# A two-layer graph network: one more graph's queries in seven products, and the row of sums kept in its accumulator

## The chip, the cores and the metric

The kernel runs on one core of one Trainium2 chip, as a single launch. The metric is the device time in microseconds (us). The kernel before takes 2637.73 us, the median of 3 runs (2637.07 to 2638.66). All data are 32-bit floats.

## The reference, cut to what matters

There are B = 16 graphs of N = 1024 nodes with C = 256 features, 4 heads of 64, and one adjacency matrix for all.

```
# layer 0, per graph, on h = max(layernorm(x), 0)
c    = mean over the features of h                        # one number per node
A    = abs(abs(sigmoid(c_m - c_n) - 0.5) - 0.5) * 2       # 1024 x 1024
Wg   = adj * A                                            # weighted graph
g    = relu((h^T @ Wg) * para)                            # queries, 256 x 1024
k, v = split(h @ kv_w)
x    = x + softmax(q k^T * scale) v                       # 4 heads
# layer 1, on h = max(layernorm(x), 0)
A_hat = (adj + I) scaled by rsqrt of the degrees on both sides
out  = batchnorm(relu(batchnorm(A_hat h W1^T + b1)) W2^T + b2)
x    = x + out
```

The batch normalisations take their statistics over all graphs, so the last product waits until all graphs are through.

## The kernel before, in words

**Order.** The program is written out by hand, in one order, and each engine takes its instructions in that order. `attention()` (L969) walks through the graphs. A graph has 16 *steps*: two halves of the features (k), two halves of the nodes (f), and four groups of two tiles each. A k and f together are a *unit* of four steps. In a step `scores()` (L863) makes two pairs of score products, and ScalarE takes their exponentials into p (L879); `Unit.add` (L892) sums p into `acc` on VectorE; `Unit.values` (L903) multiplies the p of the step before with the values. Behind the last group of a unit comes `Unit.sums` (L923): TensorE sums `acc` over the partitions by a product with ones (L929), ScalarE copies the result to an SBUF tile `row` (L931), GpSimd's queue sends two rows of it to DRAM (L932) and loads them back with the nodes on the partitions (L937, two loads). `finish` (L941) and `add_output` (L952) turn the unit's output, take the reciprocal of those sums (L955), multiply and add to x. They come two steps after the sums, three in graph 0.

**Background.** Beside the attention of graph b runs `background(b)` (L775), a generator of *pieces*. A piece of four products costs 1.71 by the planner's count. After each step the planner takes pieces until their cost has reached a due value, which grows by the total divided by 16 in each step (in graph 0, 50.0 in all, 3.125 per step). `weave(main, *sides)` (L137) runs one slot of each side generator behind each piece of the main one, from a given piece on; sides left over when the main one ends run at once. `double` (L147) runs two slots at a time. `soon` puts an action off by one piece.

**What background(0) does.** It transposes h of graph 1 (`transposed`, L374), makes keys and values (`keys_values`, L602, four pieces for k and four for v), and the weighted graph by `weigh(1)` (L408): eight tiles w, each two Abs (L439) and one Tanh (L447) on ScalarE and one multiplication with adj on VectorE (L426). A tile's slots come in pairs. Then the queries of graph 1: `plain_queries` (L568) multiplies all of h with all of w, 32 products of 128 x 128 x 512 in 16 pieces, and VectorE multiplies by para (L593). For the graphs from 2 on `queries` (L467) does it with seven half-size products, Strassen's scheme in Winograd's form, in 14 pieces: VectorE combines parts of h (`combine`, L459), subtracts tiles of w from each other in place (`take`, L501) between the products, and combines the results. Its temporary s1 sits in a tag "s1" with one buffer, which `degrees` uses for its diagonal tiles db too (L222).

**Beside the queries of graph 1** run two sides. `degrees` (L213) loads eight row tiles of adj_t, takes row sums on ScalarE (L221) and diagonals on VectorE (L223, L224), and ends with a power on GpSimd. `graph` (L232) prepares the seven pieces of adj + I for layer 1, wholly on GpSimd: for each of eight units two loads on GpSimd's queue (L247), four subtractions (L266 to L271), three DMAs to DRAM (L273 to L275). It takes two tiles of the tag "y" per unit; that tag has four buffers, and `row` (L930) is of the same tag.

**After it** come `differences(2)`, the rest of `keys_values(1)` and `prepare(2)`. In the later graphs the background also has layer 1's `aggregate` and `hidden`. TensorE's bank tag "mm" has two buffers, "sc" two, "acc" two, "p" four, "adj" three.

Of the kernel before, what the change touches and what calls it, by code (L numbers as in the profile page):

```python
# [17 lines left out]
P = 128  # L18
# [5 lines left out]
def gnn_two_layers_kernel(  # L24
# [61 lines left out]
    def layers(shifted):  # L86
# [126 lines left out]
        def degrees():  # L213

            nc.vector.tensor_reduce(row, rows.rearrange("p q t -> p t q"), AX.X, ALU.add)
            ahead = [load_adj_t(t, "at") for t in range(2)]
            yield 0.0
            for t in range(NT):
                a = ahead[t]
                blk = a[:, t * P : (t + 1) * P]  # L220
                nc.scalar.activation(a, a, AF.Copy, accum_out=col[:, t : t + 1])  # L221
                db = p1.tile([P, P], F32, tag="s1", name=f"db_{t}")  # L222
                nc.vector.tensor_mul(db, blk, ident)  # L223
                nc.vector.tensor_reduce(diag[:, t : t + 1], db, AX.X, ALU.add)  # L224
                if t + 2 < NT:
                    ahead.append(load_adj_t(t + 2, "at"))
                yield 0.0
            nc.vector.tensor_add(deg, col, row)
            nc.vector.tensor_sub(deg, deg, diag)
            rsqrt(dinv, deg, 1.0, tmp_deg)  # L230
# [159 lines left out]
        def differences(b):  # L390


            cbc = p1.tile([P, N], F32, tag="cbc", name=f"cbc_{b}")
            cbcs[b] = (
                cbc.rearrange("p (t q) -> p t q", t=NT)
                if b == 0
                else cbc.rearrange("p (q t) -> p t q", t=NT)
            )
            weighers[b] = weigh(b)
            if b == 0:  # L400
                broadcast_row(cbc, columns_of(csums[b], f"c{b}"), f"c{b}")
                return
            nc.sync.dma_start(out=csum_d[b].rearrange("(p t) -> p t", p=P), in_=csums[b])
            nc.sync.dma_start(
                out=cbc, in_=csum_d[b].rearrange("(o n) -> o n", o=1).to_broadcast([P, N])
            )
# [161 lines left out]
        def plain_queries(b):  # L568

            h = hs["a", b]  # L570
            qs[b] = [p4.tile([P, N], F32, tag="q", name=f"q_{b}_{k}") for k in range(CC)]
            for q in range(NH):
                cols = slice(q * FB, (q + 1) * FB)
                pgs = [bank(f"pg_{b}_{q}_{k}") for k in range(CC)]
                paras = []
                for k in range(CC):
                    paras.append(p2.tile([P, FB], F32, tag="para", name=f"para_{b}_{q}_{k}"))
                    nc.sync.dma_start(out=paras[k], in_=para[k * P : (k + 1) * P, cols])
                for th in range(NP):
                    i = q * NP + th  # L580
                    for k in range(CC):
                        for j in range(TH):
                            t = th * TH + j
                            product(
                                pgs[k],
                                h[:, t, k * P : (k + 1) * P],
                                weighted[b][i][:, j, :],
                                t == 0,
                                t == NT - 1,
                            )  # L590
                        if th == NP - 1:
                            dst = qs[b][k][:, cols]
                            nc.vector.tensor_mul(dst, pgs[k], paras[k])  # L593

                            soon(
                                lambda dst=dst: nc.scalar.activation(
                                    dst, dst, AF.Relu, scale=SCALE
                                )
                            )
                        yield 1.71  # L600

        def keys_values(b):  # L602
            ht = hts[b]
            ks[b] = [p4.tile([P, N], F32, tag="k", name=f"k_{b}_{k}") for k in range(CC)]
            for g in range(NH):
                for j in range(CC):
                    cols = slice(g * FB, (g + 1) * FB)
                    pk = bank(f"pk_{b}_{j}_{g}")
                    for k in range(CC):
                        product(  # L610
                            pk, kvw[:, k, j * P : (j + 1) * P], ht[k][:, cols], k == 0, k == CC - 1
                        )
                    nc.scalar.copy(ks[b][j][:, cols], pk)  # L613
                    yield 1.71

            vs[b] = [p4.tile([P, NT, P], F32, tag="v", name=f"v_{b}_{k}") for k in range(CC)]
            for g in range(NT // 2):
                pv = bank(f"pv_{b}_{g}").rearrange("p (j c) -> p j c", j=2)
                for j in range(2):
                    t = 2 * g + j  # L620
                    for k in range(CC):
                        product(
                            pv[:, j, :],
                            ht[k][:, t * P : (t + 1) * P],
                            kvw[:, k, C : 2 * C],
                            k == 0,
                            k == CC - 1,
                        )
                for k in range(CC):
                    nc.vector.tensor_copy(  # L630
                        vs[b][k][:, 2 * g : 2 * g + 2, :], pv[:, :, k * P : (k + 1) * P]
                    )
                yield 1.71
# [141 lines left out]
        def background(b):  # L775

            if b == 0:
                differences(1)
                for k in range(CC):
                    yield TOP  # L780
                    transposed(1, k)
                    yield 1.0
                w, products, norm = weighers[1], keys_values(1), Norm(2, True).all()
                yield from weave(
                    islice(products, 4), (0, double(islice(w, 8))), (0, islice(norm, 4))
                )
                yield from weave(
                    plain_queries(1), (0, norm), (0, w), (5, graph()), (7, degrees())
                )
                differences(2)  # L790
                yield from islice(products, 2)
                yield from prepare(2, products)
                return
            before = hidden(b - 1)
            gather = aggregate(b - 1)
            if b + 1 < B:
                w, products, norm = weighers[b + 1], keys_values(b + 1), normed(b - 1)
                yield from weave(islice(products, 4), (0, islice(w, 4)))
                if b == 1:
                    load_later()  # L800
                yield from weave(queries(b + 1), (0, double(w)), (9, islice(norm, 5)))
                yield next(gather)
                yield from weave(products, (0, norm))
            else:
                yield from weave(endings.pop(), (2, normed(b - 1)))
                yield next(gather)
            if b + 2 < B:
                yield from weave(gather, (3, summed(b + 2)))
                yield from prepare(b + 2, before)
            elif b + 2 == B:  # L810

                yield from gather
                endings.append(before)
            else:
                yield from gather
                yield from weave(before, (0, normed_last()))
# [66 lines left out]
        class Unit:  # L883
# [39 lines left out]
            def sums(self):  # L923

                u = self.index
                pt = ps_t.tile([P, FB], F32, tag="t", name=f"sums_{self.name}")
                for e in range(2):
                    r = slice(e * HD, (e + 1) * HD)
                    nc.tensor.matmul(pt[r, :], ones, self.acc[:, e, :], start=True, stop=True)  # L929
                row = py.tile([P, FB], F32, tag="y", name=f"row_{self.name}")  # L930
                nc.scalar.copy(row, pt)  # L931
                nc.gpsimd.dma_start(  # L932
                    out=sums_d[u], in_=row.rearrange("(e r) c -> e r c", r=HD)[:, 0, :]
                )
                self.inv = p2.tile([P, FB // P, 2], F32, tag="inv", name=f"inv_{self.name}")
                for e in range(2):
                    nc.gpsimd.dma_start(  # L937
                        out=self.inv[:, :, e], in_=sums_d[u][e].rearrange("(j q) -> q j", q=P)
                    )
# [459 lines left out]
```

## Time and profile before

| | |
|---|---|
| median of 3 runs | 2637.73 us |
| profiled execution | 2634.44 us |
| its span | 2632.6 us |
| granted TensorE clock, mean | 0.99 |
| GpSimd's DMA issue L932, each | 0.59 us, x64 |
| GpSimd's DMA issue L937, each | 0.77 us, x128 |
| VectorE's subtraction of w tiles, L501 | 1.22 us, x112 (14 graphs of 8) |
| VectorE's product with para in plain queries, L593 | 0.68 us, x8 (2 graphs of 4) |
| attention of graph 0 on TensorE | 61.5 to 197 us |

The profile is one execution. In a group's line stand the source line, the engine, the operation, the tiles it writes and reads, its shapes and count, then the busy time in us, the mean in ns of one, and the idle time of the engine just before it with what ended most of it. A line of a timeline gives the start, the length (of several merged, from the first's start to the last's end), the instruction, and in brackets the idle time before it. A product in 32-bit floats shows as two matmul records for each half of the columns, so a piece of the queries is eight records. PE is TensorE, DVE VectorE, ACT ScalarE, POOL GpSimd, SP SyncE.

### The profile page before, as it was taken

The page shows a single profiled execution, that of the slowest core. Times are in us where ns is not written, and L with a number is a line of the kernel's source. Part 1 is how long each engine was busy: PE and PEld are TensorE (multiplying, and loading weights), DVE is VectorE, ACT ScalarE, POOL GpSimd, SP SyncE. Part 2 cuts the span into 40 slices and gives each one's busy share as a digit, 9 for nine tenths or more (in the row PEclk, how much of TensorE's full clock was granted, in tenths as well). Part 3 has the DMA queues.
Part 4 walks back from the last instruction along what each step waited for, and adds up shares of the span by engine and source line. Part 5 has one row for each costly group of instructions (what it writes and reads, how often), then busy time and mean ns, then how long its engine had stood idle before and what let it go on. Part 6 is the DMA issues. An engine that isn't in the chain of part 4 may idle for free. (4 is left out here: it accounts for less than half of the span.)

```text
span 2632.6 us, 31894 instructions
## 1 busy us (share of the span) xinstructions
PE 2555.9 (97%) x11754; PEld 937.9 (36%) x11754; DVE 1725.3 (66%) x2736; ACT 1440.5 (55%) x1905; POOL 547.9 (21%) x648
## 2 busy tenths in 40 slices
PE   8979999999999999999999999999999999999995
PEld 3333333333333333333333333333333333334443
DVE  5647575766757675757667575757576675557675
ACT  5756464737364564647374645556464744335544
POOL 1361111011111111110111111111111112036653
PEclk9999999999999999999999999999999999999997
DMA  4463415252433324152524343342425233455559
GB/s 162 136 214 104 153 61 181 84 179 82 152 101 141 104 97 148 59 186 77 180 81 152 101 150 102 109 135 66 176 73 180 81 137 97 132 196 207 193 182 378
DMA packets 137188, 364.02 MB, mean 138 GB/s; under 512 B 21440, under 2 KB 38336, under 8 KB 130880
## 3 DMA queue, kind: packets, MB, share of 16 engines
q1 hardware_dynamic: 110272, 282.70, 31.5%
q0 software_dynamic: 26752, 79.20, 8.7%
q8 instruction: 95, 1.56, 0.3%
q14 instruction: 69, 0.57, 0.1%
HBM read 287.06 MB, written 74.78 MB: 137 GB/s over the span
## 5 line engine op out<-in xcount | busy, mean ns | idle before, releaser
L879 ACT ACTIVATE p<-sc 128x1024 f32<-128x1024 f32 x512 | 495.0, 1020 | 470.3 <-PE sc L871 464.1
L901 DVE TENSOR_TENSOR acc<-acc,p 128x1024 f32<-128x1024 f32 x384 | 470.8, 1226 | 222.4 <-ACT p L879 202.1
L871 PE MATMUL sc<-q,k 64*128 64x512 f32 x2048 | 511.4, 618 | 14.3 <-ACT p L879 14.3
L912 PE MATMUL o<-p,v 128*64 128x512 f32 x2048 | 497.0, 606 | 0.0
L160 PE MATMUL pg<-w,h_a 128*64 128x512 f32 x1600 | 358.1, 592 | 3.6 <-ACT k L613 1.9
L160 PE MATMUL pa<-aht,h_b 128*64 128x512 f32 x1536 | 343.5, 592 | 0.0
L871 PEld LDWEIGHTS sc<-q,k 64*128 64x128 f32 x2048 | 176.2, 186 | 336.8 <-issue 278.7
L439 ACT ACTIVATE w<-cbc,csum 128x512 f32<-128x512 f32 x256 | 293.5, 1198 | 0.0
L932 POOL DMA_DIRECT2D sums_d<-row x64 | 37.6, 587 | 1199.8 <-ACT row L931 1199.8
L160 PE MATMUL py<-at,w 128*64 128x512 f32 x1024 | 230.4, 592 | 0.0
L912 PEld LDWEIGHTS o<-p,v 128*64 128x64 f32 x2048 | 124.6, 136 | 294.6 <-issue 293.9
L426 DVE SCALAR_TENSOR_TENSOR w<-w,adj 128x1024 f32<-128x1024 f32 x128 | 157.9, 1234 | 89.2 <-ACT w L447 85.2
L160 PEld LDWEIGHTS pg<-w,h_a 128*64 128x64 f32 x1600 | 115.6, 137 | 231.7 <-issue 216.9
L160 PEld LDWEIGHTS pa<-aht,h_b 128*64 128x64 f32 x1536 | 110.4, 137 | 213.3 <-issue 201.0
L726 ACT ACTIVATE y<-py,vec 128x512 f32<-128x512 f32 x128 | 87.7, 685 | 149.0 <-PE py L160 125.1
L730 DVE BATCH_NORM_STATS2 stats<-y 128x6 f32<-128x512 f32 x128 | 85.5, 687 | 86.2 <-ACT y L726 86.2
L898 DVE TENSOR_TENSOR acc<-p,p 128x1024 f32<-128x1024 f32 x64 | 78.9, 1232 | 92.3 <-ACT p L879 92.3
L447 ACT ACTIVATE w<-w 128x1024 f32<-128x1024 f32 x128 | 135.2, 1056 | 1.8
L501 DVE TENSOR_TENSOR w<-w,w 128x1024 f32<-128x1024 f32 x112 | 132.9, 1218 | 1.5
L727 POOL DMA_DIRECT2D y_d<-y x128 | 70.2, 549 | 303.3 <-ACT y L726 302.1
L937 POOL DMA_DIRECT2D inv<-sums_d x128 | 98.4, 772 | 147.0 <-issue 63.3
L160 PEld LDWEIGHTS py<-at,w 128*64 128x64 f32 x1024 | 74.2, 137 | 145.2 <-issue 139.5
(151 smaller groups left out, 2822.0 us busy)
## 6 DMA issues: line engine op xcount, KB each, us to landing
aht<-aht_d SPq DMA_DIRECT2D x224, 512.0 KB, 6.3
adj<-in_adj_dram SPq DMA_DIRECT2D x128, 512.0 KB, 4.2
y_d<-y POOLq DMA_DIRECT2D x128, 256.0 KB, 2.6
yin_f<-y_d SPq DMA_DIRECT2D x32, 1024.0 KB, 6.3
x<-in_x_dram SPq DMA_DIRECT2D x32, 512.0 KB, 5.0
para<-in_para_dram SPq DMA_DIRECT2D x64, 256.0 KB, 3.9
x_d<-x POOLq DMA_DIRECT2D x16, 1024.0 KB, 10.4
xo_f<-x_d SPq DMA_DIRECT2D x32, 512.0 KB, 8.6
```

What stands on the lines that cost most here:

```text
L160: nc.tensor.matmul(dst[r], left[:, r], right, start=start, stop=stop)
L426: nc.vector.scalar_tensor_tensor(w, w, 1.0, a, op0=ALU.add, op1=ALU.mult)
L439: nc.scalar.activation(w[:, t, :].rearrange("p (t q) -> p t q", q=P), cbc[:, q * NT // NH : (q + 1) * NT // NH], AF.Abs, bias=csum[:, th * ...
L447: nc.scalar.activation(made[i], made[i], AF.Tanh, scale=-0.5 / C)
L501: nc.vector.tensor_sub(block(i)[part], block(x)[part], block(y)[part])
L726: nc.scalar.activation(y, made, AF.Identity, bias=b1[:, j : j + 1])
L730: nc.vector.bn_stats(stats1[:, j, i, :], y)
L871: nc.tensor.matmul(sc[:, e, :], ks[b][k][r, m * P : (m + 1) * P], qs[b][k][r, f * FB : (f + 1) * FB], start=True, stop=True,)
L879: nc.scalar.activation(pr, sc, AF.Exp)
L901: nc.vector.tensor_add(self.acc, self.acc, pr)
L912: nc.tensor.matmul(self.o[r, :], vs[b][k][:, m, r], pr[:, e, :], start=(m == 0), stop=(m == NT - 1),)
L937: nc.gpsimd.dma_start(out=self.inv[:, :, e], in_=sums_d[u][e].rearrange("(j q) -> q j", q=P))
```

## The change

Three things change, in two places.

1. In `background(0)` the queries of graph 1 are made by `queries(1)` in place of `plain_queries(1)`: seven half-size products in 14 pieces, with their combinations on VectorE and two copies on ScalarE.
2. The weighted graph of graph 1 runs further ahead: its generator gets two slots behind each of the two transposes, then eight beside the four k pieces as before, and two (not one) per piece of the queries. `degrees` starts beside the fourth piece (3), not the eighth (7), `graph` beside the fifth (4), not the sixth (5). The slot order among the sides changes: w now comes ahead of the norm.
3. In `Unit.sums`, for all 64 units, the copy of the sums goes to the first half of `acc`, which has just been summed, and no "y" tile is taken. The DMA reads it there.

```diff
             if b == 0:
                 differences(1)
+                w, products, norm = weighers[1], keys_values(1), Norm(2, True).all()
                 for k in range(CC):
                     yield TOP
                     transposed(1, k)
                     yield 1.0
-                w, products, norm = weighers[1], keys_values(1), Norm(2, True).all()
+                    yield from islice(w, 2)
                 yield from weave(
                     islice(products, 4), (0, double(islice(w, 8))), (0, islice(norm, 4))
                 )
                 yield from weave(
-                    plain_queries(1), (0, norm), (0, w), (5, graph()), (7, degrees())
+                    queries(1), (0, double(w)), (0, norm), (3, degrees()), (4, graph())
                 )
...
                     nc.tensor.matmul(pt[r, :], ones, self.acc[:, e, :], start=True, stop=True)
-                row = py.tile([P, FB], F32, tag="y", name=f"row_{self.name}")
+                row = self.acc[:, 0, :]
                 nc.scalar.copy(row, pt)
```

## The prediction

> **What bounds the kernel now.** I first read the page's busy times and slices. TensorE is the bound over the whole span, but one slice among the early ones shows 7.
>
> ```profile
> PE 2555.9 (97%) x11754; PEld 937.9 (36%) x11754; DVE 1725.3 (66%) x2736; ACT 1440.5 (55%) x1905; POOL 547.9 (21%) x648
> ...
> PE   8979999999999999999999999999999999999995
> ...
> POOL 1361111011111111110111111111111112036653
> ```
>
> The slice with 7 (132 to 197 us) is the one in which POOL shows 6: graph 0's attention, beside which the second graph's queries, the degrees and `graph()` run. That is where both edits act. Next I cut it into windows of 8 us (columns: window, then length, busy PE, PEld, DVE, ACT and POOL, granted clock, DMA share, GB/s).
>
> ```profile
> 132.00:140.00 8.00, 8.00 (x38) 2.61 (x36) 0.00 (x0) 1.10 (x2) 6.65 (x11) 1.00 0.80 309
> ...
> 172.00:180.00 8.00, 0.84 (x8) 0.29 (x4) 0.00 (x0) 0.50 (x2) 7.44 (x12) 0.69 0.56 198
> 180.00:188.00 8.00, 6.93 (x24) 2.78 (x24) 5.54 (x7) 7.97 (x9) 6.49 (x9) 0.67 0.35 120
> ```
>
> From 172 to 180 everything stands but POOL. The timelines of ACT, PE, DVE and POOL say why (start, length, instruction, in brackets the idle time before it and what ended it):
>
> ```profile
> 138.90 0.59 ACT L931 COPY row<-sums 128x512 f32<-128x512 f32 x1 [8.93 <-DMA aht_d<-two]
> ...
> 179.50 0.59 ACT L931 COPY row<-sums 128x512 f32<-128x512 f32 x1 [13.40 <-POOL two L266]
> ```
> ```profile
> 162.68 1.08 PE L929 MATMUL sums<-acc,ones 128*64 128x512 f32 x4 [2.46 <-DVE acc L901]
> ...
> 181.06 3.79 PE L871 MATMUL sc<-q,k 64*128 64x512 f32 x8 [8.22 <-ACT p L879]
> ```
> ```profile
> 158.15 0.20 DVE L955 RECIPROCAL inv<-inv 128x8 f32<-128x8 f32 x1 [6.00 <-DMA inv<-sums_d]
> ```
> ```profile
> 143.46 0.58 POOL L932 DMA_DIRECT2D sums_d<-row  x1
> 151.38 1.56 POOL L937 DMA_DIRECT2D inv<-sums_d  x2 [7.34 <-DMA sums_d<-row]
> ...
> 185.44 0.64 POOL L932 DMA_DIRECT2D sums_d<-row  x1
> 187.43 1.54 POOL L937 DMA_DIRECT2D inv<-sums_d  x2 [1.35 <-DMA sums_d<-row]
> ```
>
> There are two chains. One: the copy of a unit's sums to `row` waits for a "y" buffer that `graph()` holds; the exponentials queue behind it on ACT, the scores behind those. Two: the sums' DMAs and the inverses' loads are queued on POOL behind `graph()`; DVE's reciprocal waits for them, the sums of p behind it, TensorE behind those. TensorE's idle gaps from 140 to 196 us are 1.69+0.33+2.46+8.22+0.48+0.76 = 13.9 us, and the lower clock makes the scores at 181 us 1.8 us longer than the usual 1.99 and the transposes behind them 0.3. From 196 us on it is full: windows of 160 us hold 159.6 to 159.8 busy until the attention's end.
>
> **What the Trainium skill says.** "TensorE: Matmul & The Clock Gate", Specifications: ScalarE, VectorE and GpSimdE are strict FIFO; the waits above agree. Same page, "What's actually happening": an idle window halves the clock; here it falls to 0.69 and 0.67 after the 8.22 us. "SBUF — State Buffer", "Who interferes with whom": a DVE instruction with two SBUF inputs and a GpSimd one that reads SBUF share a port pair, and the second to issue blocks fully. It agrees: beside L901 a L267 took 1.59 us instead of 0.73. "DMA: Bandwidth & Descriptors", "Anatomy of one DMA — SWDGE (gpsimd) path": some 2 us fixed, mostly the write receipt. Here `sums_d` lands in 1.7 us where it is quiet, in 7.6 behind `graph()`'s writes.
>
> **The change, part by part.** I number graph 0's attention in steps (one pair of score groups, then the values of the step before) and the unit sums by unit: sums 0 come in step 4, sums 1 in 8, sums 2 in 12, sums 3 in step 16. Three steps after its sums a unit needs its inverses. The planner's due is 3.125 per step.
>
> *Two pieces fewer.* Queries take 14 pieces in place of 16; two pieces are 3.60 us in PE's timeline (pg x16). So graph 0's pieces end about one step sooner.
>
> *DVE and ACT beside it.* Added: 8 subtractions of w by 1.22 (L501), 2 combinations by 0.69, 11 sums and differences by 0.69, 4 L487 by 0.68; removed: 4 L593 by 0.68. Net 9.8+1.4+7.6 = 18.7 us of DVE, and two copies (0.48 each in sequence) on ACT. From 76 to 140 us DVE is busy 32 of 64, and the later graphs carry the same work without a gap on PE, so this I cost at nothing on DVE. If the cover fails, DVE's lag lands on the wait for the inverses.
>
> *The weighted graph earlier.* Two pairs of slots move to steps 1 and 2, all the rest to Q0, Q1 and Q2. A pair is 3.35 us of ACT (2.39+0.96). ACT up to the exponentials of step 4: from 67.05 (end of step 1's) come 8 pairs 26.8, exponentials of steps 2 and 3 3.7, four k copies 1.9, three pairs of relu 3.5, two new copies 0.95: 103.9 against 101.46 now. So sums 0's copy comes 2.45 us later. TensorE's waits in steps 2 to 5 become 1.0+2.0+3.4+1.5 against 1.06+1.87+2.33; it runs about 2 us late by step 6. The moved loads of adj sit on SP, before para and `at`; cbc landed by 63.5 us, in time. The next graph's cbc and adj loads come to stand on SP two pieces earlier, near 146 to 158 us, beside `sums_d` 1: its landing stays as slow as now. `degrees()` and `graph()` start at pieces 3 and 4, not 7 and 5; at step 5 POOL still has the loads of inverses 0 ahead of them, so `graph()` starts at 108.23+2.45 = 110.7.
>
> *The copy into acc.* ACT no longer waits (8.93 and 13.40 us gone), nor do the exponentials. The copy itself costs the same. It holds an acc buffer until the DMA has read it, where it was free after TensorE's sums; the next user is the unit after next, four steps later, and for unit 1 that first sum (step 12) stands on DVE behind the inverses of unit 1 anyway, which land after `sums_d` 1. So nothing; if that cover were gone, the wait would be `sums_d`'s landing. Nothing else in the kernel waits for "row" (L931 elsewhere waits for its sums, at most 0.3 us).
>
> *What is late next.* POOL. Its chain is not shortened by the copy. Sums 1 (step 8) now come with `graph()`'s unit 5, not 4, behind them in POOL's queue: five units ahead in place of four. In this order:
> - units 0 to 3: 111.3 to 143.46 now, so +2.45 and half a collision: 146.4
> - unit 4: 6.4 now, 7.1 with a collision: 153.5
> - `sums_d` 1: landing 3 to 7.6 us after issue, I take 5.5: 159.0; loads of the inverses 1.56: 160.6; the second lands 5 after its start: 165 (161 to 167)
>
> TensorE has reached sums 2 at about 159.7 (its solid run to 142.6, K5 to 148.2, two steps). DVE stands from step 11 with everything behind the reciprocal: add_output 1.85, two sums 2.5; sums 2 start at 169 to 170. So TensorE waits about 10 us here in place of 2.46. On POOL goes on:
> - unit 5 8.3 (10.2 now with two collisions), unit 6 7.1, unit 7 5.7, the degrees' power 2.3, one collision 1: 185.0
> - `sums_d` 2, its landing, both loads: second load starts at 187.8, lands 3.1 later: 190.9
> - add_output 1.85, two sums 2.5: **sums 3 at 195.2**, now 198.35
>
> TensorE and ACT alone would be there at 192.5: from 170 come sums and K8 (4.5 at the low clock), the three slots and exponentials on ACT to 179, 183.4 and 187.4, then scores, transposes and values. The later of the two counts: 198.35-195.2 = 3.1 us gained. After sums 3 both kernels have the same work, all of it on a full TensorE, so the 3 us stay.
>
> **Sum.** The profiled execution took 2634.44 (span 2632.6 and 1.8 around it); 2631.4 after. The median of the runs is 3.3 us above that execution, so 2637.7-3.1 = 2634.6. About 0.2% (5.3 us) is what a measurement of this kernel tells from no change.
>
> **Rivals.** *Full credit*: the gaps vanish and nothing takes their place: 13.9+2.1 idle and slow clock, 3.6 of pieces, less 2.5 of new ACT waits: 17.1 us, 2620.6. For it: ACT's waits are the larger ones named. Against it: POOL is busy from 108 to 185 us almost without a gap, and DVE waits for what hangs on it. A weaker form (POOL's landings short) stops at the TensorE path, 2632.
>
> *POOL longer* (slower): 18.7 us more of two-input DVE work runs while POOL subtracts. Each collision costs POOL about 0.95. Now 5.6 us of its chain are collisions. With every second of its 32 subtractions hit it is 15.2, 9.6 more: sums 3 6.5 later than now, 2644.2. It decides from 3 us of additional collisions on. For it: units 0 to 2 lie beside a DVE that is 79% busy and show one collision each. Against: that is one in four, not two; and DVE stands while it waits for inverses 1.
>
> *Not what it says*: `degrees()` takes its diagonal tile from the same single buffer ("s1") that queries() uses until its third product. If DVE's queue waits for that product, it is 1 to 3 us in step 5, covered by the later stall: 2634 to 2637.
>
> **How the numbers follow.** Forecast (POOL's chain pins sums 3, -7 to +2): 0.62. Full credit or its weaker form: 0.2. POOL longer: 0.13. The last: 0.05. Landing of `sums_d` 1 (3 to 7.6) moves the end by -2.5 to +2, collisions by -2 to +3; ACT's order by 1. The range reaches part of the way into both rivals: 2625 to 2642. Faster by over 0.2% takes full credit and the forecast's quick end: 0.31; slower half of POOL longer and a tail: 0.11; within: 0.58.
>
> **What would show it.** Right: L931 waits for its sums alone; the reciprocals of units 1 and 2 wait some 14 and several us for inv<-sums_d; sums 2 wait for acc by about 10 us near 160; POOL's `graph()` ends near 185; PE's slice stays 7 or 8. Wrong: `graph()` ends well before 180 or after 190; the reciprocals wait little; a new wait on DVE's subtractions of w or on `at` ahead of a product.

## The result and the profile after

The changed kernel takes 2643.73 us (median of 11 runs, 2642.87 to 2645.37) against 2637.67 for the one before (11 runs): ratio 1.0025, 95% interval 1.0017 to 1.0033. It is slower by 6.1 us. The forecast was 3.1 us faster, with 2642.0 as the upper end. The profiled execution took 2645.37 us, 10.9 more than the one profiled of before; that one lay 3.2 below its own median, this one 1.6 above, so of the differences read in the two traces some 5 us belong to the choice of executions.

The page of the changed kernel, the same slices: TensorE's dip is still there, now an 8 and a 7.

```profile
PE 2561.8 (97%) x11738; PEld 940.3 (36%) x11738; DVE 1749.7 (66%) x2757; ACT 1441.8 (55%) x1907; POOL 554.6 (21%) x648
...
PE   8879999999999999999999999999999999999995
...
POOL 1381111111111111111111111111111112026653
```

Its windows of 8 us (columns as before) show VectorE full up to 148 us, then two stretches (from 164 and from about 199 us) in which TensorE and ScalarE stand most of the time while POOL works, or only its DMAs land.

```profile
116.00:124.00 8.00, 8.00 (x40) 2.78 (x38) 7.86 (x6) 5.57 (x9) 7.88 (x11) 1.00 0.71 241
...
140.00:148.00 8.00, 8.00 (x44) 2.95 (x42) 7.83 (x10) 1.04 (x2) 7.88 (x12) 1.00 0.51 183
...
164.00:172.00 8.00, 1.23 (x6) 0.14 (x2) 2.33 (x6) 0.00 (x0) 5.80 (x9) 0.86 0.20 51
172.00:180.00 8.00, 4.95 (x20) 2.48 (x20) 5.96 (x8) 3.80 (x6) 7.88 (x10) 0.50 0.59 201
...
196.00:204.00 8.00, 4.59 (x20) 1.18 (x16) 2.45 (x6) 2.52 (x3) 1.56 (x2) 0.99 0.15 36
```

The timelines of TensorE, VectorE and POOL of the changed kernel:

```profile
175.05 1.98 PE L930 MATMUL sums<-acc,ones 128*64 128x512 f32 x4 [9.82 <-DVE acc L902]
...
205.88 1.98 PE L930 MATMUL sums<-acc,ones 128*64 128x512 f32 x4 [5.29 <-DVE acc L902]
```
```profile
169.54 0.20 DVE L956 RECIPROCAL inv<-inv 128x8 f32<-128x8 f32 x1 [13.91 <-DMA inv<-sums_d]
...
201.41 0.20 DVE L956 RECIPROCAL inv<-inv 128x8 f32<-128x8 f32 x1 [6.38 <-DMA inv<-sums_d]
```
```profile
157.55 0.58 POOL L933 DMA_DIRECT2D sums_d<-acc  x1
166.08 1.56 POOL L938 DMA_DIRECT2D inv<-sums_d  x2 [7.95 <-DMA sums_d<-acc]
...
187.87 1.71 POOL L266 TENSOR_TENSOR two<-au_f 128x256 f32<-128x256 f32 x1
189.66 1.59 POOL L267 TENSOR_TENSOR two<-au_f,two 128x256 f32<-128x256 f32 x1
...
194.70 0.57 POOL L933 DMA_DIRECT2D sums_d<-acc  x1
197.94 1.56 POOL L938 DMA_DIRECT2D inv<-sums_d  x2 [2.67 <-DMA sums_d<-acc]
```

ScalarE's copy of the sums waits no longer for a "y" buffer. What came in its place is what the forecast named: the inverses come late through POOL's queue, VectorE waits for them, TensorE for VectorE. But sums 3 start at 205.88 us, not at the 195.2 of the forecast, and 7.5 us later than the 198.35 of before. The lower clock after that wait adds 2.4: from sums 3 to the next graph's queries it is 13.9 us at a mean granted clock of 0.83, and 11.5 us at 1.00 before, with TensorE busy throughout in both. The queries of graph 2 start at 219.80 against 209.86.

A table of POOL's chain in graph 0 helps with what follows. I worked it out from POOL's timelines. "Collisions" is what its operations took over their shortest durations (0.73 us for a subtraction), "waits" the idle time before operations and loads of `graph()` that a DMA ended. The length runs from the first load of `graph()` to the end of its last DMA's issue. In the rows with the earlier starts (changed, the seven products, plain queries) it holds the power of the degrees, some 2 us on POOL, which in the other two rows comes behind it.

| kernel | graph() starts | length | collisions | waits | landing of sums_d 1, from issue to POOL's next | sums 3 on PE |
|---|---|---|---|---|---|---|
| before | 108.2 | 74.8 | 5.7 | 4.8 | 7.9 | 198.35 |
| changed | 111.2 | 83.6 | 11.8 | 4.6 | 8.5 | 205.88 |
| copy in acc alone | 107.5 | 83.0 | 12.7 | 11.0 | 3.2 | 202.37 |
| seven products, row in y | 110.3 | 75.9 | 7.4 | 7.3 | 2.9 | 202.44 |
| changed, plain queries | 110.0 | 80.6 | 5.5 | 13.5 | 2.9 | 202.10 |

The column of the landing needs a word. In every row `sums_d` 1 stands directly behind the writes of a unit (unit 3 with the old starts, unit 4 with the new), so the writes alone do not tell 8.5 from 2.9. In the changed kernel SP's queue had just issued the loads of `cbc` and of three tiles of adj for the next graph, and they landed beside it (in the kernel before, loads of `at` did):

```profile
152.66 0.33 SPq L404 DMA_DIRECT2D cbc<-csum_d  x1
153.08 37.98 SPq L172 DMA_DIRECT2D adj<-in_adj_dram  x5
```

With the row in y these loads start at 161.6, behind that landing; in the two other rows with 2.9 and 3.2 no transfer from SP's queue was in flight at that time. No run moved these loads alone.

### The profile page after: what moved, and what is told of

Same layout as the page of the kernel before. It is cut to its first block, busy times and chain, and to the rows that moved or that the text cites. A ratio compares the mean times of both kernels' runs of the same rounds, so it can differ in the third digit from the quotient of the medians.

```text
span 2643.2 us, 31883 instructions
## 1 busy us (share of the span) xinstructions
PE 2561.8 (97%) x11738; PEld 940.3 (36%) x11738; DVE 1749.7 (66%) x2757; ACT 1441.8 (55%) x1907; POOL 554.6 (21%) x648
## 3 DMA queue, kind: packets, MB, share of 16 engines
q1 hardware_dynamic: 110272, 282.70, 31.3%
## 4 chain that ended last, share of the span: by engine, by line
PE 83%; DVE 6%; DMA 4%; POOL 3%; ACT 2%; issue 1%; SPq 0%; POOLq 0%; DVEq 0%
PE sc L872 16%; PE o L913 16%; PE pa L160 15%; PE pg L160 11%; PE py L160 8%; PE m_f L1195 7%; PE pk L160 4%; PE pv L160 2%; DMA out_dram<-xo_f 2%; PE sums L930 2%; DVE acc L902 2%; PE ot L948 1%; PE htp L385 1%; DVE q L529 1%; ACT w L439 1%
## 5 line engine op out<-in xcount | busy, mean ns | idle before, releaser
L160 PE MATMUL pg<-w,h_a 128*64 128x512 f32 x1568 | 350.7, 592 | 3.6 <-ACT k L613 1.9
L933 POOL DMA_DIRECT2D sums_d<-acc x64 | 37.5, 586 | 1204.2 <-ACT acc L932 1204.2
L160 PEld LDWEIGHTS pa<-aht,h_b 128*64 128x64 f32 x1536 | 110.3, 137 | 213.3 <-issue 200.7
L501 DVE TENSOR_TENSOR w<-w,w 128x1024 f32<-128x1024 f32 x120 | 145.7, 1244 | 1.5
```

Of the source, the lines that this page charges most:

```text
L160: nc.tensor.matmul(dst[r], left[:, r], right, start=start, stop=stop)
L501: nc.vector.tensor_sub(block(i)[part], block(x)[part], block(y)[part])
```

## The experiments

Two theories stood at the outset. Q: POOL's queue, with the sums' DMAs behind `graph()`, sets the end. V: VectorE is late by its own new work. All ratios are against the kernel before, timed on the chip of that run; the chips differ between groups of runs, so a difference of two experiments is less sharp than either ratio.

**e1. All of graph 0's sums on SP's queue.**

```diff
+                issue = nc.sync if self.at[0] == 0 else nc.gpsimd
-                nc.gpsimd.dma_start(out=sums_d[u], ...)
+                issue.dma_start(out=sums_d[u], ...)
...
-                    nc.gpsimd.dma_start(out=self.inv[:, :, e], ...)
+                    issue.dma_start(out=self.inv[:, :, e], ...)
```

> The changed kernel, with the three DMAs of a unit's sums (L933 and the two of L938) issued from SP's queue in graph 0. Theory Q (POOL's queue: the loads of the inverses stand behind graph()'s units, and VectorE behind them): the reciprocals of units 1 and 2 no longer wait, the sums of unit 3 start near 183 us in place of 205.9, and the kernel takes about 2622 us, faster than both. Theory V (VectorE itself is late by the 18.7 us of work that the seven products added): the waits for acc stay, 2642 to 2645 us.

2631.62 us, ratio 0.9979 (0.9972 to 0.9986). It beats both kernels: the reciprocals wait for no DMA any more, and sums 3 start at 191.15. But it is 9 us short of what Q expected. SP's queue too is worked off in its order: loads of `at` stand behind the sums of unit 0, which wait for ScalarE's copy, and ScalarE then waits 13.0 us for `at` (8.0 in e5 below, which leaves unit 0 on POOL and is 5 us faster). Part of the wait had moved to another queue.

**e2. The copy in acc alone, on the kernel before.**

```diff
-                row = py.tile([P, FB], F32, tag="y", name=f"row_{self.name}")
+                row = self.acc[:, 0, :]
```

> The kernel before, with the copy of the sums into acc alone. Theory Q: the copy's waits on ScalarE vanish, but POOL's chain is as long as before, the reciprocal of unit 2 now waits for it until about 191 us, and the sums of unit 3 start near 196 in place of 198.4: 2635 us, a gain of 2 to 3. Theory V: nothing on VectorE is added, so the whole of the gaps comes back: 2625 to 2628 us.

2641.65 us, ratio 1.0014 (1.0006 to 1.0022): slower, where both theories had it faster. This falls on my assumption that POOL's chain stays as long as it was. It grew from 74.8 to 83.0 us, though no work was added anywhere. While ScalarE stood before its copy (8.93 us up to 138.90 in the kernel before), VectorE stood too, and with VectorE the loads of `at` that wait for its diagonals. POOL then ran alone: in the window from 132 to 140 us VectorE was busy for 0.00 us, here, in the same window of e2, for 4.25.

```profile
132.00:140.00 8.00, 8.00 (x38) 2.36 (x34) 4.25 (x7) 4.33 (x8) 5.59 (x7) 1.00 0.83 278
```

In e2 POOL has 12.7 us of collisions in place of 5.7, and 11.0 us of DMA waits in place of 4.8; the faster landing of `sums_d` 1 gives 4.7 back. So ScalarE's waits are gone, and VectorE's wait for POOL's queue is there in their place:

```profile
166.49 1.98 PE L929 MATMUL sums<-acc,ones 128*64 128x512 f32 x4 [9.25 <-DVE acc L901]
...
202.37 1.97 PE L929 MATMUL sums<-acc,ones 128*64 128x512 f32 x4 [9.61 <-DVE acc L901]
```

Where did the chain grow? Units 2 and 3 of `graph()`, which had run beside the stop, took 22.0 us in place of 15.9. The traces of e6 and e9 below say the same: 18.9 us in e6, where the copy does not wait, and 13.6 in e9, where it does. The wait that was taken away had been giving POOL's chain room there. But nearly as much, 5.4 us, was added in units 0 and 1, ahead of the wait: they took 24.8 us, 19.4 in the trace of before. That is not the work of the copy. Most of it is one load of `graph()`, which waited for a write to land (in order: before, e2, e9):

```profile
121.63 1.46 POOL L247 DMA_DIRECT2D au_f<-in_adj_t_dram  x2
```
```profile
126.45 1.46 POOL L247 DMA_DIRECT2D au_f<-in_adj_t_dram  x2 [3.19 <-DMA aht_d<-au_f]
```
```profile
126.88 1.46 POOL L247 DMA_DIRECT2D au_f<-in_adj_t_dram  x2 [3.23 <-DMA aht_d<-au_f]
```

In e9 the first sums that go elsewhere are those of unit 1, which come later than this load, and its units 0 and 1 took 24.4 us. So the traced execution of before, which was 3.2 us faster than its median, had these units short. How often it does is not known, since only one execution of it was traced.

**e3. The seven products alone** (the changed kernel with `row` in a y tile again, the edit of e2 reversed).

> The changed kernel with row in a y tile as before. Theory Q: POOL's chain is as long as in the changed kernel and ends the stage whether ScalarE waits or not: 2643 to 2648 us. Theory V: the copy's waits on ScalarE come on top of VectorE's lateness: 2653 to 2658 us.

2639.06 us, ratio 1.0008 (0.9999 to 1.0016): hardly to be told from no change, and faster than Q expected. The copy's wait is back (18.8 us once). The chain is 7.7 us shorter than in the changed kernel: `sums_d` 1 lands 5.6 us faster and there are 4.4 us less of collisions, against 2.7 more of DMA waits.

**e4. Plain queries in the changed kernel** (`queries(1)` replaced by `plain_queries(1)`, all else as changed).

> The changed kernel with plain_queries(1) in place of queries(1), all else as changed (weighted graph ahead, degrees and graph at pieces 3 and 4, the copy in acc). Theory Q: TensorE has 3.6 us more to do, which is covered; POOL's units lose most of their collisions with VectorE's subtractions, the chain ends some 5 us sooner: 2637 to 2640 us. Theory V: 18.7 us less on VectorE, the waits for acc vanish: 2628 to 2632 us.

2640.49 us, ratio 1.0014 (1.0007 to 1.0020), close to Q's range and far from V's. Collisions fall from 11.8 to 5.5 and `sums_d` 1 lands 5.6 us faster, but the DMA waits rise from 4.6 to 13.5, so the chain is only 3 us shorter.

**e8. graph() one piece later** (`(4, graph())` to `(5, graph())`), so that unit 4 comes behind sums 1.

> The changed kernel with graph() from piece 5 on, as before, so that unit 4 comes behind the sums of unit 1 on POOL. Theory Q: the reciprocal of unit 1 comes some 8 us sooner, but POOL's whole work ahead of the sums of unit 2 is the same, so the sums of unit 3 start within 2 us of 205.9: 2642 to 2646 us. If it is unit 1's late inverse that costs the time: 2635 to 2638 us.

2640.02 us, ratio 1.0009 (1.0000 to 1.0017): between the two. Inverses 1 come 9.2 us sooner (160.33 in place of 169.54); sums 3 start 4.2 us sooner, since `sums_d` 1 lands faster and fewer operations collide. The queue's order is worth some 4 us.

**e7. No reads by POOL in graph().** Its four subtractions become memsets, which read nothing; the additions of the identity (L261) stay, and still read.

```diff
-                sub(two[:, 0], b12, a[:, 0, 0])
-                sub(two[:, 1], b22, two[:, 0])
+                for _ in range(3):
+                    nc.gpsimd.memset(two, 0.5)
...
-                sub(b12, b22, b12)
-                sub(one, b21, two[:, 1])
+                nc.gpsimd.memset(a[:, 0], 0.5)
+                nc.gpsimd.memset(one, 0.5)
```

> The changed kernel, in which graph()'s four subtractions per unit are replaced by five memsets of 256 to 512 elements on GpSimd (it leaves out the combinations of the adjacency matrix's quarters, so layer 1 works on other numbers). Its queue, DMAs and number of units are the same; its operations read nothing from SBUF. Theory Q with collisions on the shared port: no stretched operation on POOL, graph() 12 to 15 us shorter (83.6 us now, about 70), the sums of unit 3 near 192: 2628 to 2634 us. If its DMA waits make the length instead: graph() 78 us or more and 2638 to 2642 us.

2628.28 us, ratio 0.9964 (0.9951 to 0.9978), as expected with collisions; sums 3 start at 191.64. Every memset takes its usual time, wherever VectorE works:

```profile
114.48 1.69 POOL L266 MEMSET two<- 128x512 f32 x3
...
174.69 1.68 POOL L266 MEMSET two<- 128x512 f32 x3
```

From the first load of `graph()` to the issue of `sums_d` 2 it is 69.7 us (109.58 to 179.27), 83.5 in the changed kernel: 13.8 less, of which some 3 are the shorter memsets (2.5 against 2.9 us per unit) and 11 the collisions. The landing of `sums_d` 1 is as slow here as in the changed kernel, 9.3 us, with SP's loads beside it again. The Trainium skill ("SBUF — State Buffer", "Who interferes with whom") has VectorE's two-input instructions contend with a GpSimd instruction that reads SBUF, not with one that only writes it; these runs agree.

**e5 and e6. Units 1 and 2 alone on SP**, e5 on the changed kernel, e6 on that of e2 (plain queries, old order, copy in acc).

```diff
+                issue = nc.sync if u in (1, 2) else nc.gpsimd
```

> The changed kernel with the sums' DMAs of units 1 and 2 alone on SP's queue; unit 0's stay on POOL, so the loads of the row tiles for degrees() are not held up on SP as they were with all of graph 0's on SP. Theory Q: nothing waits for POOL in graph 0; the sums of unit 3 start near 185 us (191 with all on SP): 2622 to 2628 us. Theory V: as with all on SP or slower, 2631 us or more.

> The kernel before with the copy into acc, and the sums' DMAs of units 1 and 2 on SP; plain queries and the old starts. Theory Q: the gap left by the copy alone closes, 2625 to 2632 us, and the seven products are then worth their two pieces (3.6 us) less some 2 us of waits on ScalarE: 0 to 4 us more than with the changed queries. Theory V: without VectorE's extra work it is faster than the same with the seven products, 2618 to 2622 us.

e5 takes 2626.27 us, ratio 0.9957 (0.9944 to 0.9971); e6 2618.31, ratio 0.9928 (0.9914 to 0.9942). e5 meets Q. e6 beats Q's range and falls on V's: with the queue out of the way, the seven products with their order cost 8.0 us, where I had put them at a gain of up to 4. POOL's collisions are about 14 us in e6, more than in the changed kernel, and cost it nothing that shows: only sums 3 are queued behind them, and their reciprocal does not wait. TensorE's timeline of e6 in 140 to 195 us shows one gap:

```profile
177.24 2.04 PE L871 MATMUL sc<-q,k 64*128 64x512 f32 x8 [0.25 <-ACT p L879]
```

In e5 the scores wait 2.71 us and then run at a lower clock, and a transpose waits 3.82:

```profile
149.81 3.44 PE L872 MATMUL sc<-q,k 64*128 64x512 f32 x8 [2.71 <-ACT p L880]
...
176.84 1.97 PE L385 MATMUL htp<-ident,h_a 128*128 128x128 f32 x8 [3.82 <-DVE ht L388]
```

**e9. Only units 1 and 2 on SP**, on the kernel before, `row` a y tile.

> The kernel before, with the sums' DMAs of units 1 and 2 on SP and nothing else; row stays a y tile. If the two waits are in series (ScalarE for a y tile that graph() holds, then VectorE for POOL's queue), freeing the queue alone leaves ScalarE's waits of 8.9 and 13.4 us: the sums of unit 3 near 195 us, 2632 to 2637 us, against 2618.3 with the copy into acc as well. If the queue alone is the cause, and the copy worth nothing: about 2619 us.

2632.23 us, ratio 0.9984 (0.9977 to 0.9991), as expected for waits in series. ScalarE's copy waits twice, though the second wait is shorter than in the kernel before:

```profile
142.22 0.58 ACT L931 COPY row<-sums 128x512 f32<-128x512 f32 x1 [12.72 <-DMA aht_d<-two]
...
175.14 0.58 ACT L931 COPY row<-sums 128x512 f32<-128x512 f32 x1 [6.17 <-DMA aht_d<-two]
```

So on the kernel before the copy in acc costs 4 us by itself, the queue gains 5 by itself, and both together gain 19: the two waits are in series, and each hides what the other would bring.

**e10. Plain queries in e5.**

> The changed kernel with plain_queries(1) in place of queries(1) and the sums' DMAs of units 1 and 2 on SP: between the two runs of 2626.3 (seven products) and 2618.3 us (plain, old order), it has the new order of the weighted graph and the early starts, but not the seven products. If the seven products' work on VectorE makes the 8 us: 2618 to 2621 us. If the new order (ScalarE's waits in steps 3 to 5, degrees and graph earlier) makes them: 2624 to 2627 us.

2621.21 us, ratio 0.9942 (0.9928 to 0.9955). Of the 8.0 us between e5 and e6, 5.1 are the seven products and 2.9 the new order; with intervals of some 3.5 us to either side the split is rough.

**e11. e5 with the memsets of e7.**

> The changed kernel with the sums' DMAs of units 1 and 2 on SP, and memsets in place of graph()'s subtractions (it leaves out the combinations of the adjacency matrix's quarters). If VectorE is late in the seven products because its two-input instructions collide with POOL's, the scores of steps 11 and 12 no longer wait and it takes 2618 to 2621 us, 2626.3 with the collisions. If it is late by its own 18.7 us of work: 2624 us or more.

2619.90 us, ratio 0.9935 (0.9922 to 0.9949): the 5.1 us and a little more come back when POOL reads nothing. So the work that the seven products add does not make VectorE late by itself; it does so together with the collisions. (`graph()` also ends some 10 us sooner in e11, but no sums wait for it in either run.) The same pairs of instructions in VectorE's timeline of e5:

```profile
118.03 4.58 DVE L501 TENSOR_TENSOR w<-w,w 128x1024 f32<-128x1024 f32 x2
...
141.30 4.34 DVE L902 TENSOR_TENSOR acc<-acc,p 128x1024 f32<-128x1024 f32 x2
```

and of e11 (its lines are numbered one lower):

```profile
118.23 2.35 DVE L500 TENSOR_TENSOR w<-w,w 128x1024 f32<-128x1024 f32 x2
...
137.47 2.55 DVE L901 TENSOR_TENSOR acc<-acc,p 128x1024 f32<-128x1024 f32 x2
```

From 116 to 156 us VectorE is busy 37.8 of 40 us in e5 and 33.2 in e11; TensorE 37.3 and 40.0.

## Why the prediction was wrong, step by step

- *The binding chain* was right. POOL pins sums 3, the copy's waits vanish and nothing is gained by that alone. e5 against the changed kernel (17.5 us) shows the queue's part.
- *ScalarE's order* was right, but for the last wait: TensorE waits in steps 2 to 5 for 1.10, 1.88, 3.45 and 0.34 (I said 1.0, 2.0, 3.4, 1.5), `graph()` from 111.2 (I said 110.7, and this execution began its scores 0.56 late).
- *"This I cost at nothing on DVE"* failed. My ground was that the later graphs carry the same work without a gap. They do, but beside them POOL subtracts almost nothing. In graph 0 VectorE was busy 31.3 of 32 us from 116 to 148 and ran late; e10 and e5 put a price of 5.1 us on it with the queue freed, and e11 shows that it takes the collisions to make it.
- *POOL's chain* was mis-sized, and this is the step that turned the forecast round. Units 0 to 3 ended at 148.7 (146.4), unit 4 took 8.9 (7.1), `sums_d` 1 landed 8.5 after its issue (5.5), unit 7 took 8.6 (5.7). `sums_d` 2 went out at 194.7 (185.0). Of these 9.7 us against the forecast 3.0 are the landing. I had seen that the next graph's loads would stand beside it and had called it as slow as now (7.6), and then reckoned with 5.5. Nearly all the rest is collisions: my chain kept them at about the 5.6 us of before; they were 11.8. Of the 9.3 us by which `sums_d` 2 comes later than in the kernel before, 6.1 are more collisions and 2.9 the later start. Landing, reciprocal and sums then follow nearly as reckoned (sums 3 come 11.2 us behind `sums_d` 2; 10.2 in my chain).
- *What I overlooked* shows in e2: many of the durations and waits that I took from the trace of before were those of a POOL that ran beside a stopped VectorE (units 2 and 3, and again 6 and 7). Taking away the stop changes them. I priced POOL's chain as if it did not depend on the wait that the change removes. They were also those of one execution, whose units 0 and 1 were short; this did not hurt here, since in the changed kernel they took 19.8 us, much as reckoned.
- *The rival "POOL longer"* is what happened, with its mechanism: I had every second subtraction hit, 15.2 us of collisions and sums 3 6.5 us later; it was 11.8 and 7.5. I gave it 0.13 because VectorE would stand while it waits for inverses 1; it does stand from 155.6 to 169.5, but the collisions lie before and after that. My rate of one in four came from units 0 to 2, beside a VectorE that I read as 79% busy. That share is of 108 to 132 us; over the units themselves (111.3 to 135.7) it was busy for 16.0 of 24.4 us, since most of unit 2 lies beside the stop. *Not what it says* came to 0.88 us (db waits for the third product), as harmless as I said.

Open: the traces' loss (about 9.4 us behind graph 0) is larger than the medians' 6.1. How the rest varies between executions was not followed up, and each kernel's collisions and DMA waits are known from one execution. Why one and the same load of `graph()` waits over 3 us in one execution and not in another is open too, as is what the landing of `sums_d` 1 costs by itself.

## What to carry to other kernels

A trace's durations hold for the neighbours that ran beside them. Before you take away a wait, look at which other engine had a free run during it, and price that engine's work again as if everything beside it went on. They are also those of one execution: here a stretch of the same program took 19.4 us in one trace and 24.4 in another, nearly as much as the whole change made. And where a chain passes through a queue that is full with other work, free the queue first: here the copy cost 4 us behind the full queue, and brought 14 once the two units' DMAs were on another (e9 to e6).

## What the runs showed of the hardware

- A collision of a two-input VectorE instruction with a GpSimd subtraction stretches both sides: L501 from 1.2 to about 2.3 us each at worst (e5), L266 from 0.73 to 1.71 (the changed kernel). GpSimd memsets showed none of it (e7, e11).
- A transfer of 4 KB on GpSimd's queue landed 1.7 us after issue where it was quiet (the kernel before, `sums_d` 2). Directly behind a unit's writes (896 KB) POOL's next instruction came 2.9 to 3.2 us after issue in e2, e3 and e4, and 8.5 and 9.3 us after it in the changed kernel and e7, where loads from SP's queue were in flight too.
